# Loads of a selective scan on one Trainium2 core: upper quarters ahead of lower ones, B and C by one transfer each, delta on 72 partitions

## The chip, the cores and the metric

The kernel runs on one core of one Trainium2 chip. The metric is the device time in microseconds (us) from the start to the end of one execution; lower is better. A core has a matrix engine (PE, with PEld for its weight loads), a vector engine (DVE), an activation engine (ACT), GpSimd (POOL) and a sync engine (SP). SP and ACT issue transfers (DMA) on queues of their own, and 16 DMA engines, which all queues share, move the bytes between the device memory (DRAM) and the on-chip memory of 128 partitions. PE writes its results to a second on-chip memory, PSUM[...].

## What is computed

Four layers work on four images of 64x64 positions and 96 channels. The first two layers are a selective scan: each image is projected to E = 192 channels, passed through a depthwise 3x3 convolution, and then read as a sequence of 4096 steps in K = 4 directions (by rows, by columns, and both backwards). For each direction, channel and each of N = 16 states runs a recurrence over the steps:

```
def step(h, inp):
    u, d, b, c = inp
    dA = jnp.exp(d[..., None] * A)
    h = dA * h + d[..., None] * b[:, :, None, :] * u[..., None]
    y = jnp.einsum('bken,bkn->bke', h, c)
    return (h, y)
```

`d` (delta) and `u` depend on the channel and not on the state; `b` and `c` on the state and not on the channel. The four directions' results are summed, normalised, gated and projected back. The last two layers are a linear attention and a quantised feed-forward network on the tokens; the change doesn't touch them.

## The kernel before

**Phases.** The two scan layers, for two pairs of images each, make four phases, which run one after the other. Of each phase there are three parts: a preparation (`prepare`, L148), the scan itself (`scan_phase`, L466) and an end (`finish`, L543). `run` (L696) lets the end of one phase run beside the preparation of the next; a scan phase runs alone. The token layers come last.

**What the preparation leaves in DRAM.** For each chunk of TC = 512 steps (NC = 8 chunks) `steps` (L282) computes delta, delta times u and the rows of B and C, and stores them. An index g of G = 8 stands for direction and image.

- `ph.delta`: delta as the sum of three bf16 parts (NP16 = 3), laid out part, g, channel, step.
- `ph.du`: delta times u in fp32, laid out copy, g, channel, step. There are two copies, stored by ACT's and by SP's queue (L319).
- `ph.bc`: B's and C's 16 rows each, laid out g, row, step; the store is at L301, on ACT's queue, 256 times in all.

**Partitions in the scan.** All 128 partitions hold independent recurrences: partition = 32 a + 4 g + s, where the state is 4 a + s with a and s from 0 to 3. A quarter is the 32 partitions of one a.

**A unit** is 12 channels (EB) of one chunk. A phase has 8 chunks of 16 units, 128 in all, and 12 scans per unit. For each unit:

- SP loads `h` (L381, L391), 128 partitions by 12 channels by 512 steps in fp32, from `ph.du`. Every row of the source goes to four partitions (the four s), by a broadcast in the source. It takes six transfers: for each of three groups of quarters, first channels 0 to 5 and then 6 to 11. The group `(1, 2)` is the two middle quarters, partitions 32 to 95, in one transfer from both copies (768 KB); `(0, 1)` is the lower quarter, partitions 0 to 31, from copy 0 (384 KB), and `(3, 1)` the upper one, partitions 96 to 127, from copy 1 (384 KB). A row is 12 KB.
- SP loads `dlt` (L371), delta's parts for the 12 channels, on 24 partitions (g, part), 12 KB each (288 KB).
- POOL multiplies `h` by B in four slices of three channels (`times_b`, L403), six scans ahead.
- PE spreads one channel of delta over the 128 partitions and adds up its three parts, by a matmul with a matrix of zeros and ones, `rep` (`replicate`, L408), into PSUM; ACT applies exp with A as its scale (`decay`, L414).
- DVE runs the scan in place on `h` (L420), starting from the carry of the chunk before.
- While the next unit is being scanned, PE contracts `h` with C (`contract`, L432; the weights `cw` are made from C by ACT at L354), ACT evicts the result into `d` (L449), and SP stores it (`store`, L457) in four transfers of 48 KB.

**Order.** The scan phase is a hand-written order (`manual_schedule`), so every engine works its queue in the order of the code. On SP this is, at the end of each unit: the four stores of the unit before; then B's load for the next chunk where the unit is the ninth of its chunk, or C's load for the chunk after the next where it is the last; then `load` of the unit three ahead. `h` has four buffers, `dlt` three, B and C two. B and C are four transfers each (`load_states`, L341), one per quarter. At the start of a phase SP issues B, unit 0, C, unit 1, unit 2 and the next C; ACT makes the first 16 pieces of `cw` before its first exp.

**Constants.** `rep` is loaded once as fp32 and cast to bf16 (L94); `constants` (L902) makes it on the host. Only its first 24 rows are used.

Of the kernel before, what the change touches and what calls it, by code (L numbers as in the profile page):

```python
# [9 lines left out]
F32 = mybir.dt.float32  # L10
F16 = mybir.dt.float16
BF16 = mybir.dt.bfloat16
# [12 lines left out]
NS = 16  # L25
R = 6
K = 4
G = 2 * K
PAD = HW + 2
TC = 512  # L30
NC = L // TC
ROWS = TC // HW
EB = 12
NEB = E // EB
ER = EB // 4
PITCH = 2
NP16 = 3
XD = 2 * NS + R + 1
XD2 = 64 + XD
HID = 384  # L40
# [40 lines left out]
class Consts:  # L81
# [9 lines left out]
        self.eps = pool.tile([128, 1], F32, name="eps")  # L91
        self.nc.vector.memset(self.eps, EPS)

    def scans(self, pool):  # L94
        rep = self.load(pool, "rep", [128, 128])
        self.rep = pool.tile([128, 128], BF16, name="rep16")
        self.nc.vector.tensor_copy(self.rep, rep)
        self.perm = self.load(pool, "perm", [128, K, 128])
        self.unit = self.load(pool, "unit", [128, 128])
        self.gmask = self.load(pool, "gmask", [128, G])  # L100
        self.group = self.load(pool, "group", [C, C])
        self.one_row = self.load(pool, "one_row", [XD2, 1])
# [25 lines left out]
class Scans:  # L128
    def __init__(self, tc, ctx, cst, a):
        nc = self.nc = tc.nc  # L130
        self.tc, self.cst, self.a = tc, cst, a

        def pool(name, bufs, **space):
            return ctx.enter_context(tc.tile_pool(name=name, bufs=bufs, **space))

        self.dram = pool("stage", 2, space=DRAM)
        self.keep = pool("keep", 2)
        cst.scans(pool("const_s", 1))

    def bank(self):  # L140
        return self.p_c.tile([128, TC], F32, name="c")
# [6 lines left out]
    def prepare(self, ph):  # L148

        nc, cst, a, pre = self.nc, self.cst, self.a, ph.pre  # L150
        ph.gs = self.keep.tile([C, 2, 2], F32, name="gs", bufs=3)
        ph.delta = [
            self.dram.tile([NP16, G, E, TC], BF16, name="delta", bufs=2 * NC) for _ in range(NC)
        ]


        ph.du = [
            self.dram.tile([2, G, E + PITCH, TC], F32, name="du", bufs=2 * NC) for _ in range(NC)
        ]
        ph.bc = [self.dram.tile([G, 2 * NS, TC], F32, name="bc", bufs=2 * NC) for _ in range(NC)]  # L160
        ph.ud = self.dram.tile([C, 2, HW, 2, 64], F32, name="ud")
        ph.y = self.dram.tile([64, G, 2, 2, NEB, 16 * EB], F32, name="y")
        x = ph.x_in[ph.pair]

        with self.tc.tile_pool(name="prep", bufs=1) as wp, self.tc.tile_pool(
            name="steps", bufs=2
        ) as sp:

            def load(name, shape, at=0):
                t = wp.tile([at + shape[0]] + shape[1:], F32, name=name)  # L170
                nc.sync.dma_start(t[at:], a[pre + name])
                return t

            xp = load("x_proj", [C, 2, 2, XD2])
            dt_w = load("dt_w", [XD2 - 2 * NS, 2, E], at=2 * NS)
            conv_b = load("conv_b", [C, 2])
            ds = load("Ds", [C, 2, K])
            dsum = wp.tile([C, 2], F32, name="dsum")
            nc.vector.tensor_reduce(dsum, ds, mybir.AxisListType.X, ALU.add)
            yield  # L180


            st = wp.tile([C, 2, 8, 6], F32, name="st")
            with self.tc.tile_pool(name="stats", bufs=2) as rp:
                for hl in range(8):
                    raw = rp.tile([C, 8, 2, 64], F32, name="raw")
                    nc.sync.dma_start(raw, x[:, hl * 8 : hl * 8 + 8])
                    for i in range(2):
                        nc.vector.bn_stats(st[:, i, hl], raw[:, :, i])
                    yield  # L190
            for i in range(2):
                mv = wp.tile([C, 2], F32, name="mv")
                nc.vector.bn_aggr(mv, st[:, i].rearrange("p c s -> p (c s)"))
                ps = self.bank()
                nc.tensor.matmul(ps[:C, :1], cst.group, mv[:, 0:1], start=True, stop=True)
                gs = ph.gs[:, i]
                nc.vector.tensor_copy(gs[:, 0:1], ps[:C, :1])
                d = wp.tile([C, 1], F32, name="d")
                nc.vector.tensor_tensor(d, mv[:, 0:1], gs[:, 0:1], ALU.subtract)
                nc.vector.scalar_tensor_tensor(d, d, d, mv[:, 1:2], ALU.mult, ALU.add)  # L200
                ps = self.bank()
                nc.tensor.matmul(ps[:C, :1], cst.group, d, start=True, stop=True)
                ln = wp.tile([C, 2], F32, name="ln")
                neg_rsqrt(nc, cst, ps[:C, :1], ln[:, 0:1], gs[:, 1:2], ln[:, 1:2])
                nc.vector.tensor_scalar_mul(gs[:, 1:2], gs[:, 1:2], -1.0)
                yield
            in_w = wp.tile([C, E], F32, name="in_w")
            nc.sync.dma_start(in_w, a[pre + "in_proj_w"][:, :E])
            taps = wp.tile([C, 9, E], F32, name="taps")
            nc.sync.dma_start(taps, a[pre + "conv_w"].unsqueeze(0).broadcast_to([C, 9, E]))  # L210

            nc.vector.tensor_tensor(
                taps, taps, in_w.unsqueeze(1).broadcast_to([C, 9, E]), ALU.mult
            )

            xc = [wp.tile([C, 2, L], F32, name="xc", bufs=2) for _ in range(2)]
            yield from self.convolve(ph, 0, x, xc[0], taps, conv_b, dsum)
            ph.beside = 0.5
            other = self.convolve(ph, 1, x, xc[1], taps, conv_b, dsum)
            for i in range(2):  # L220
                for c in range(NC):
                    for k in range(2):
                        yield from self.steps(ph, sp, xc[i], xp, dt_w, i, k, c)
                        for _ in range(2):
                            next(other, None)
                            yield
                for _ in other:
                    yield
                ph.beside = 1.7
# [52 lines left out]
    def steps(self, ph, sp, xc, xp, dt_w, i, k, c):  # L282


        nc, cst = self.nc, self.cst
        u = scan_view(xc, k, c)
# [3 lines left out]
        xd = sp.tile([XD2, TC], F32, name="xd")  # L290

        nc.scalar.activation(xd[:XD], ps[:XD], AF.Identity, bias=cst.one_row[:XD])  # L292
        nc.scalar.activation(
# [4 lines left out]
        for back in range(2):  # L298
            at = 64 * back
            g, cc = 2 * (k + 2 * back) + i, NC - 1 - c if back else c  # L300
            nc.scalar.dma_start(ph.bc[cc][g], xd[at : at + 2 * NS])  # L301
            both.append((g, cc, scan_view(xc, k + 2 * back, cc), self.p_d.tile([C, 2, TC], F32, name="d")))
        for m in range(2):
            for back, (_, _, _, ps) in enumerate(both):
# [5 lines left out]
        for g, cc, u, ps in both:  # L310
            delta = sp.tile([C, 2, TC], F32, name="dl")
            parts = sp.tile([C, NP16, 2, TC], BF16, name="parts")
            du = sp.tile([C, 2, TC], F32, name="du_sb")
# [24 lines left out]
        ph.carry = self.keep.tile([128, E], F32, name="carry")  # L338
        ph.b, ph.c, ph.cw = {}, {}, {}

    def load_states(self, t, of):  # L341

        for a in range(4):
            self.nc.sync.dma_start(t[32 * a : 32 * a + 32], of[:, 4 * a : 4 * a + 4])

    def load_b(self, ph, c):
        ph.b[c] = self.units.tile([128, TC], F32, name="b")
        self.load_states(ph.b[c], ph.bc[c][:, :NS])

    def load_c(self, ph, c):  # L350
        ph.c[c] = self.units.tile([128, TC], F32, name="c")
        self.load_states(ph.c[c], ph.bc[c][:, NS:])

    def weights(self, ph, c, op):  # L354

# [15 lines left out]
    def load_delta(self, u):  # L371

        nc, ph = self.nc, u.ph
        u.dl = self.units.tile([NP16 * G, EB, TC], BF16, name="dlt", bufs=3)
        at = u.eb * EB
        nc.sync.dma_start(
            u.dl.rearrange("p e t -> p (e t)"),
            ph.delta[u.c][:, :, at : at + EB].rearrange("n g e t -> g n (e t)"),
        )

    def load(self, u):  # L381

        nc, ph = self.nc, u.ph
        u.h = self.units.tile([128, EB, TC], F32, name="h", bufs=4)
        self.load_delta(u)
        n = EB // 2
        for first, quarters in ((1, 2), (0, 1), (3, 1)):
            for e in range(0, EB, n):
                self.load_quarters(u, e, n, first, quarters)

# [17 lines left out]
    def replicate(self, u, n):  # L408

        u.a[n] = self.p_a.tile([128, TC], F32, name="a")  # L410
        rep = self.cst.rep[: NP16 * G]
        self.nc.tensor.matmul(u.a[n], rep, u.dl[:, n], start=True, stop=True)  # L412

    def decay(self, u, n):  # L414
        at = u.eb * EB + n
# [486 lines left out]
def constants():  # L902

    p = np.arange(128)
    q = np.arange(C)
    rep = (p[:, None] % 32 < NP16 * G) & (p[:, None] % 32 // NP16 == p[None, :] // 4 % G)
    gmask = p[:, None] // 4 % G == np.arange(G)[None, :]


# [74 lines left out]
```

## Time and profile before

Three runs took 12473.74 to 12504.42 us, with a median of 12483.95 us. The profiled execution took 12443.48 us, and its span from the first to the last instruction is 12441.7 us.

| what | value |
|---|---|
| median of three runs | 12483.95 us |
| profiled execution, its span | 12443.48 us, 12441.7 us |
| PE busy | 10107.0 us (81%) |
| DVE busy | 9376.9 us (75%) |
| POOL busy | 7386.0 us (59%) |
| ACT busy | 7185.6 us (58%) |
| the scan on DVE (L423), with and without carry | 6356.7 + 869.6 us |
| B's product on POOL (L406) | 7016.6 us, 3456 ns each |
| the spreading matmul (L412), its weight load | 551 ns, 101 ns each |
| exp on ACT (L416) | 4030.3 us, 662 ns each |
| SP's queue: bytes, packets | 2163.38 MB, 552496 |
| ACT's queue: bytes, packets | 306.26 MB, 328704 |

The shares are means over the whole execution. The four scan phases take up 1909, 1911, 1912 and 1928 us of the span, and the preparations, ends and token layers, in which other engines and other lines set the pace, lie between and after them. The matrix clock is granted at full or at half speed in turn; it averages 0.665 over the span and 0.60 in the scan phases. A busy PE isn't PE at its peak. Idle time of an engine that isn't the bound costs nothing.

### The profile page before, as it was taken

What the parts mean: (1) busy time and instruction counts of PE and PEld (TensorE: products, weight loads), DVE (VectorE), ACT (ScalarE), POOL (GpSimd) and SP (SyncE); (2) the same over time, 40 slices, a digit from 0 to 9 for tenths busy, and PEclk for the clock granted to TensorE, in tenths of its full rate; (3) what the DMA queues carried; (4) which work ended last, traced back from release to release, by engine and by line L of the source; (5) the groups of instructions that cost most, each with busy time, mean ns of one, the idle gap of its engine ahead of it and who ended that gap; (6) DMA issues with size and microseconds to landing.
All of it is one profiled execution on the core that took longest, in us unless ns stands there. A gap on an engine that the chain in (4) does not pass through costs nothing.

```text
span 12441.7 us, 340858 instructions
## 1 busy us (share of the span) xinstructions
PE 10107.0 (81%) x147008; PEld 4972.1 (40%) x147008; DVE 9376.9 (75%) x9235; ACT 7185.6 (58%) x11815; POOL 7386.0 (59%) x2316
## 2 busy tenths in 40 slices
PE   7758888879878888879878888888878888887777
PEld 2224444433334444433334444443334444444333
DVE  2479999963569999982469999992459999993567
ACT  2456666644456666653456666663446666662556
POOL 0159999950149998960139899880129989990000
PEclk8665565669675555659775656558776655557787
DMA  3567676754667676764566777664567666663110
GB/s 92 172 227 247 244 248 247 248 168 140 213 205 246 245 247 244 250 200 128 176 215 244 246 247 249 243 226 125 174 202 249 244 243 245 245 244 122 30 21 11
DMA packets 882704, 2491.45 MB, mean 200 GB/s; under 512 B 279058, under 2 KB 561840, under 8 KB 737456
## 3 DMA queue, kind: packets, MB, share of 16 engines
q1 hardware_dynamic: 552496, 2163.38, 50.6%
q10 hardware_dynamic: 328704, 306.26, 8.5%
q8 instruction: 1158, 18.97, 0.7%
q14 instruction: 346, 2.83, 0.1%
HBM read 1955.42 MB, written 513.80 MB: 198 GB/s over the span
## 4 chain that ended last, share of the span: by engine, by line
DMA 53%; PE 20%; SPq 8%; DVE 7%; ACT 4%; issue 4%; POOL 3%; ACTq 1%; POOLq 0%; DVEq 0%
DMA h<-du 47%; PE c L260 8%; SPq L396 7%; POOL h L406 3%; PE f L591 2%; DVE h L423 2%; PE d L306 2%; DMA yk<-y 1%; PE c L289 1%; PE f L600 1%; POOL parts L320 1%; PE f L682 1%; DMA du<-du_sb 1%; PE y L441 1%; DVE parts L321 1%
## 5 line engine op out<-in xcount | busy, mean ns | idle before, releaser
L406 POOL TENSOR_TENSOR h<-h,b 128x1536 f32<-128x1536 f32 x2048 | 7016.6, 3456 | 780.6 <-DMA h<-du 369.0
L423 DVE TENSOR_TENSOR_SCAN h<-a,carry,h 128x512 f32<-128x512 f32 x5376 | 6356.7, 1259 | 391.8 <-POOL h L406 360.9
L416 ACT ACTIVATE a<-a,a_col 128x512 f32<-128x512 f32 x6144 | 4030.3, 662 | 1966.6 <-PE a L412 1814.4
L441 PEld LDWEIGHTS y<-h,cw 128*32 128x32 f32 x131072 | 2886.3, 145 | 3597.6 <-issue 1606.1
L441 PE MATMUL y<-h,cw 128*32 128x48 f32 x131072 | 3702.1, 269 | 438.0 <-ACT a L416 216.9
L412 PE MATMUL a<-dlt,rep 24*128 24x512 bf16 x6144 | 3319.4, 551 | 884.8 <-DVE h L423 782.1
L320 POOL CAST parts<-dl 96x1024 bf16<-96x1024 f32 x256 | 341.3, 1348 | 3092.1 <-DVE dl L317 2785.6
L316 DVE TENSOR_TENSOR du_sb<-dl,xc 96x1024 f32<-96x1024 f32 x256 | 397.3, 1577 | 1296.2 <-ACT dl L314 1234.8
L453 ACT COPY d<-y 128x384 f32<-128x384 f32 x2048 | 979.6, 478 | 485.7 <-PE y L441 432.7
L260 PE MATMUL c<-xn,taps 96*96 96x512 f32 x2304 | 1034.1, 609 | 73.5 <-DVE xn L245 71.0
L423 DVE TENSOR_TENSOR_SCAN h<-a,h 128x512 f32<-128x512 f32 x768 | 869.6, 1201 | 189.0 <-ACT a L416 110.6
L412 PEld LDWEIGHTS <-rep 24*128 24x128 bf16 x6144 | 471.9, 101 | 903.6 <-issue 451.0
L306 PE MATMUL d<-xd,dt_w 7*96 7x512 f32 x1024 | 520.8, 859 | 254.9 <-ACT xd L292 225.6
L260 PEld LDWEIGHTS c<-xn,taps 96*96 96x96 f32 x2304 | 382.6, 167 | 707.5 <-issue 628.7
L823 POOL MEMSET tn<- 1x4096 f32 x8 | 27.8, 3506 | 865.0 <-PE pa L843 514.7
L267 ACT ACTIVATE xc<-c,conv_b 96x512 f32<-96x512 f32 x128 | 87.3, 682 | 718.1 <-PE c L260 633.2
L591 PE MATMUL f<-yk,perm 128*128 128x384 f32 x1024 | 415.9, 546 | 99.6 <-DMA yk<-y 88.8
L314 ACT ACTIVATE dl<-d 96x1024 f32<-96x1024 f32 x256 | 252.0, 1017 | 400.9 <-DMA delta<-parts 234.5
L321 DVE TENSOR_TENSOR parts<-dl,parts 96x1024 bf16<-96x1024 f32 x256 | 366.9, 1455 | 153.2 <-POOL parts L320 153.1
L289 PE MATMUL c<-xc,x_proj 96*103 96x512 f32 x512 | 420.2, 958 | 4.2 <-ACT xc L267 4.2
L306 PEld LDWEIGHTS d<-xd,dt_w 7*96 7x96 f32 x1024 | 151.7, 212 | 542.4 <-ACT xd L292 295.8
L360 ACT ACTIVATE cw<-c,gmask 128x256 f32<-128x256 f32 x512 | 287.9, 573 | 126.2 <-DMA h<-du 65.9
(114 smaller groups left out, 5650.6 us busy)
## 6 DMA issues: line engine op xcount, KB each, us to landing
h<-du SPq DMA_DIRECT2D x1024, 768.0 KB
h<-du SPq DMA_DIRECT2D x2048, 384.0 KB
delta<-parts ACTq DMA_DIRECT2D x512, 288.0 KB
dlt<-delta SPq DMA_DIRECT2D x512, 288.0 KB
du<-du_sb SPq DMA_DIRECT2D x256, 384.0 KB
du<-du_sb ACTq DMA_DIRECT2D x256, 384.0 KB
y<-d SPq DMA_DIRECT2D x2048, 48.0 KB
yk<-y SPq DMA_DIRECT2D x256, 384.0 KB
```

The costliest lines, as they stand in the source:

```text
L260: nc.tensor.matmul(rows(ps[:C]), taps[:, tap, h * C : (h + 1) * C], xn[:, ROWS * c + dy : ROWS * (c + 1) + dy, dx : dx + HW], start=tap == ...
L289: nc.tensor.matmul(rows(ps[:XD2]), xp[:, k, h], u[:, h], start=h == 0, stop=h == 1)
L306: nc.tensor.matmul(ps[:, m], dt_w[part, k, m * C : (m + 1) * C], xd[part], start=True, stop=True)
L321: nc.vector.tensor_tensor(parts[:, 2], delta, parts[:, 1], ALU.subtract)
L396: self.nc.sync.dma_start(u.h[32 * first : 32 * (first + quarters), e : e + n].rearrange("p e t -> p (e t)"), source.rearrange("a g e t -> ...
L406: self.nc.gpsimd.tensor_tensor(h, h, b, ALU.mult)
L412: self.nc.tensor.matmul(u.a[n], rep, u.dl[:, n], start=True, stop=True)
L416: self.nc.scalar.activation(u.a[n], u.a[n], AF.Exp, scale=u.ph.a_col[:, at : at + 1])
L423: self.nc.vector.tensor_tensor_scan(u.h[:, n], u.a.pop(n), u.h[:, n], 0.0 if u.c == 0 else u.ph.carry[:, at : at + 1], ALU.mult, ALU.add,)
L441: self.nc.tensor.matmul(view(u.y[32 * j : 32 * j + 32], l2 * EB, (8 * EB, 4), (1, EB)), u.ph.cw[u.c][:, l1, 8 * j + l2], view(u.h, 64 * l1 ...
L453: self.nc.scalar.copy(u.d[:, :, :, l1], u.y[:, : 32 * EB].rearrange("p (t h x) -> p t h x", t=4, h=2))
L591: nc.tensor.matmul(ps[:, : 4 * C].rearrange("p (w v e) -> p w v e", w=4, v=nv), cst.perm[:, k], view(t, off, (sw if k < 2 else -sw, 4), (1 ...
```

## The change

It has three parts.

1. `load` takes the upper quarter's two transfers before the lower quarter's.
2. `ph.bc` is laid out as groups of four rows first, then g, then the row in its group (B's four groups, then C's four), so that the 128 rows of B, and those of C, lie one after another in the order of the partitions. B and C are loaded by one transfer each in place of four. The store in the preparation (L301) writes eight pieces of four rows.
3. `dlt` is on 72 partitions: each of the 24 rows is cut in three by channel (channels 0 to 3, 4 to 7, 8 to 11), and a partition holds 4 channels, 4 KB. `rep` has 72 rows and three versions, one for each third; each has ones for that third's rows alone and zeros elsewhere. `replicate` takes the version and the column that belong to its channel. The fp32 copy of `rep` lies in a pool that is given back after the cast.

Nothing else differs: the number of computing instructions and their order are the same, and the bytes loaded into `h`, `dlt`, B and C too.

```diff
+DROWS = 3 * NP16 * G
+DC = EB // 3
...
-    def scans(self, pool):
-        rep = self.load(pool, "rep", [128, 128])
-        self.rep = pool.tile([128, 128], BF16, name="rep16")
-        self.nc.vector.tensor_copy(self.rep, rep)
+    def scans(self, tc, pool):
+        self.rep = pool.tile([DROWS, EB // DC, 128], BF16, name="rep16")
+        with tc.tile_pool(name="rep_f", bufs=1) as once:
+            rep = self.load(once, "rep", [DROWS, EB // DC, 128])
+            self.nc.vector.tensor_copy(self.rep, rep)
...
-        ph.bc = [self.dram.tile([G, 2 * NS, TC], F32, name="bc", bufs=2 * NC) for _ in range(NC)]
+        ph.bc = [self.dram.tile([NS // 2, G, 4, TC], F32, name="bc", bufs=2 * NC) for _ in range(NC)]
...
-            nc.scalar.dma_start(ph.bc[cc][g], xd[at : at + 2 * NS])
+            nc.scalar.dma_start(ph.bc[cc][:, g], xd[at : at + 2 * NS])
...
-    def load_states(self, t, of):
+    def load_states(self, ph, c, first, name):
 
-        for a in range(4):
-            self.nc.sync.dma_start(t[32 * a : 32 * a + 32], of[:, 4 * a : 4 * a + 4])
+        t = self.units.tile([128, TC], F32, name=name)
+        of = ph.bc[c][first : first + NS // 4]
+        self.nc.sync.dma_start(t, of.rearrange("a g s t -> (a g s) t"))
+        return t
 
     def load_b(self, ph, c):
-        ph.b[c] = self.units.tile([128, TC], F32, name="b")
-        self.load_states(ph.b[c], ph.bc[c][:, :NS])
+        ph.b[c] = self.load_states(ph, c, 0, "b")
 
     def load_c(self, ph, c):
-        ph.c[c] = self.units.tile([128, TC], F32, name="c")
-        self.load_states(ph.c[c], ph.bc[c][:, NS:])
+        ph.c[c] = self.load_states(ph, c, NS // 4, "c")
...
-        u.dl = self.units.tile([NP16 * G, EB, TC], BF16, name="dlt", bufs=3)
+        u.dl = self.units.tile([DROWS, DC, TC], BF16, name="dlt", bufs=3)
         at = u.eb * EB
         nc.sync.dma_start(
             u.dl.rearrange("p e t -> p (e t)"),
-            ph.delta[u.c][:, :, at : at + EB].rearrange("n g e t -> g n (e t)"),
+            ph.delta[u.c][:, :, at : at + EB].rearrange(
+                "n g (h e) t -> (n g) h (e t)", h=EB // DC
+            ),
         )
...
-        for first, quarters in ((1, 2), (0, 1), (3, 1)):
+        for first, quarters in ((1, 2), (3, 1), (0, 1)):
...
-        rep = self.cst.rep[: NP16 * G]
-        self.nc.tensor.matmul(u.a[n], rep, u.dl[:, n], start=True, stop=True)
+        h, e = divmod(n, DC)
+        self.nc.tensor.matmul(u.a[n], self.cst.rep[:, h], u.dl[:, e], start=True, stop=True)
...
-    rep = (p[:, None] % 32 < NP16 * G) & (p[:, None] % 32 // NP16 == p[None, :] // 4 % G)
+    r = np.arange(DROWS)[:, None, None]
+    third = np.arange(EB // DC)[None, :, None]
+    rep = (r % 3 == third) & (r // 3 % G == p[None, None, :] // 4 % G)
```

More of the change, by code (lines that the diff above doesn't have):

```diff
@@ L137, in __init__ @@
         self.keep = pool("keep", 2)
-        cst.scans(pool("const_s", 1))
+        cst.scans(tc, pool("const_s", 1))
     def bank(self):
```

## The prediction

> **What bounds the kernel now.** I read the chain of waits first, on the page.
>
> ```profile
> DMA 53%; PE 20%; SPq 8%; DVE 7%; ACT 4%; issue 4%; POOL 3%; ACTq 1%; POOLq 0%; DVEq 0%
> DMA h<-du 47%; PE c L260 8%; SPq L396 7%; POOL h L406 3%; PE f L591 2%; DVE h L423 2%; PE d L306 2%; DMA yk<-y 1%; PE c L289 1%; PE f L600 1%; POOL parts L320 1%; PE f L682 1%; DMA du<-du_sb 1%; PE y L441 1%; DVE parts L321 1%
> ```
>
> Nearly half of the chain is the loading of `h`, although DVE looks full. So, second, busy time in the four scan phases (columns: stretch, length, busy PE, PEld, DVE, ACT, POOL with counts, clock, DMA share, GB/s).
>
> ```profile
> 775.00:2684.00 1909.00, 1621.64 (x34042) 832.57 (x34041) 1805.52 (x1536) 1305.54 (x2268) 1740.52 (x508) 0.60 0.70 245
> 3613.00:5524.00 1911.00, 1624.24 (x34042) 833.32 (x34041) 1806.32 (x1536) 1306.72 (x2269) 1740.56 (x509) 0.60 0.70 244
> 6462.00:8374.00 1912.00, 1625.12 (x34042) 832.86 (x34041) 1806.35 (x1536) 1307.18 (x2268) 1740.75 (x508) 0.60 0.70 244
> 9307.00:11235.00 1928.00, 1626.64 (x34042) 833.21 (x34041) 1806.62 (x1536) 1307.57 (x2267) 1740.52 (x508) 0.60 0.69 242
> ```
>
> A phase has 128 units, so 14.93 us each (1911/128), of which DVE works 14.11. Its idle time over the phases is 7660 − 7225 = 435 us: the most that feeding it better can bring there. Third, where that idle time lies: DVE's timeline, then SP's.
>
> ```profile
> 1018.72 14.21 DVE L423 TENSOR_TENSOR_SCAN h<-a,carry,h 128x512 f32<-128x512 f32 x12 [1.99 <-POOL h L406]
> 1036.00 28.31 DVE L423 TENSOR_TENSOR_SCAN h<-a,carry,h 128x512 f32<-128x512 f32 x24 [3.08 <-ACT d L453]
> ...
> 1170.99 14.21 DVE L423 TENSOR_TENSOR_SCAN h<-a,carry,h 128x512 f32<-128x512 f32 x12 [2.46 <-POOL h L406]
> ```
>
> ```profile
> 1011.32 6.19 SPq L344 DMA_DIRECT2D c<-bc  x4
> ...
> 1146.86 6.19 SPq L344 DMA_DIRECT2D b<-bc  x4
> ...
> 1208.29 0.69 SPq L376 DMA_DIRECT2D dlt<-delta  x1
> 1210.16 6.89 SPq L396 DMA_DIRECT2D h<-du  x6
> ```
>
> The 12 scans of a unit run without a gap; every stop is at a unit's first scan, where POOL's product is late (the ACT named beside 3.08 is only the last semaphore seen), and the long ones (3.08, 2.46) come two units after B's or C's four issues. Fourth, what SP waits for (1000 to 2600 us: sum, times, longest).
>
> ```profile
> SPq L396 <- DMA h<-du: 419.1, 277, 4.0
> SPq L461 <- DMA h<-du: 135.6, 141, 2.8
> SPq L376 <- DMA h<-du: 118.8, 94, 2.8
> ```
>
> SP can't issue before an earlier load lands: a full set is out all the time. Yet the DMA share is 0.70. The last view, narrow windows in one unit (same columns as above), says why.
>
> ```profile
> 1208.00:1211.00 3.00, 2.20 (x55) 1.20 (x55) 3.00 (x3) 1.90 (x4) 3.00 (x1) 1.00 0.55 229
> 1211.00:1213.00 2.00, 2.00 (x62) 1.28 (x53) 2.00 (x3) 1.31 (x3) 0.85 (x2) 1.00 0.92 257
> 1213.00:1214.00 1.00, 0.20 (x2) 0.00 (x0) 1.00 (x2) 0.87 (x2) 1.00 (x1) 1.00 1.00 351
> 1214.00:1216.00 2.00, 1.04 (x33) 0.73 (x32) 1.35 (x2) 1.16 (x2) 2.00 (x2) 0.65 0.91 264
> 1216.00:1218.00 2.00, 2.00 (x42) 0.93 (x35) 2.00 (x2) 1.02 (x2) 2.00 (x1) 0.50 0.80 332
> ```
>
> Before the two-quarter loads go out (1210.16) about half of the engines work, each at 229/(0.55x16) = 26 GB/s. Then all work, but at 257/14.7 = 17.5 and 264/14.6 = 18; from 1216 they are back at 332/12.8 = 26. So many engines at once isn't the trouble; some pair of transfers is.
>
> [...] In SP's order the upper quarter is last and so still draining when the next unit's two-quarter loads start: the 4 us at 18 GB/s fit it. [...]
>
> [...] Collisions: 0.70x16x14.93 = 167 engine-us are busy, 245 GB/s x 14.93 us / 26 = 141 would do[...].
>
> **The change, part by part.**
> - Upper quarters first. Same bytes and issues. [...] Takes up to 1.6 us from a unit; nothing if I have the cause wrong.
> - `dlt`: 24 rows to 72 partitions[...].
> - B and C: four issues become one [...] about 4 us less of SP (6.19 to some 2) where the long stops are. They are a part of the 435.
> - The 72-row replicate (L412, 551 ns) and its weights (101 ns): rows cost nothing by the nearest rows (7x96 weights at L306 212 ns, 96x96 at L260 167). I take 0; the other end is in the rivals. The order of weights within a unit changes nothing; each matmul loads them now.
> - The store of B/C in the preparation (L301): [...] 0 to 40 us. DMA has room there; I take 8.
> - Start of a phase: SP spends 2.92 us on B, 4.72 on C before the second unit's load; C's landing (765.4) holds ACT's weights and the first scan (774.8). About 3 us x 4 = 12 gained, 0 to 20.
> - The constant `rep` grows to 108 KB, once: nothing.
>
> [...] What is late next: DVE itself. POOL has four products, 13.72 us (the timeline's 4 from 1197.36), and in a phase's first chunk DVE needs 13.73, so the two run level. SP's 11 issues are 7.3 us. At half clock PE takes all but 0.2 us of each three scans (3.53), 13.3 us per unit; yet the gapless scans from 1215.70 ran at clock 0.50 for their first 20 us. So DVE's idle time falls from 435 to about 40 (0.08 per unit for jitter and the level first chunk; bounds 0 and 130). Gain 435 − 40 + 12 − 8 = 399: the profiled 12443.5 becomes 12044. The runs' median lies 40 above that profile (12483.95), so 12085.
>
> **Rivals.**
> - A: collisions [...] move to the lower quarter. Then only bytes count: 0.47+0.08 less of 0.85 us idle per unit; 0.3x512 = 154 remain. Gain 435−154+4 = 285: 12200. [...] Against: full speed from 1216 with 13 engines busy.
> - B: it doesn't do what it says: [...] POOL, 0.4 us from the bound, keeps DVE waiting: some 12440-12480, no change.
> - C, slower: the 72-row replicate. If its weight load grows with rows (101 to 303 ns) and isn't hidden, PE has 13.3+12x0.2 = 15.7 us at half clock, 80% of a phase (mean 0.60), so 15.4 on average, +0.45x512 = 230: 12715. It decides from 0.135 us per replicate ((14.93−13.3)/12). Against: 7 rows load no faster than 96.
>
> **Numbers.** Main case 0.66 (12085; its own range 12030 to 12140), A 0.21, B 0.06, C 0.07. Range 12030 to 12220: main and A. A change under 0.3% (37 us) couldn't be told from none. Faster 0.89, same 0.04, slower 0.07.
>
> **What would show it.** DVE idle in a phase down from 104-121 to about 10; DMA share near 0.6 in the phases, windows at full share with 26 GB/s per engine; SP's waits for `h` loads mostly gone; `dlt` matmuls of 72 rows at the old 551 ns; phases of about 1815. Wrong if full-share windows still fall to 18 GB/s per engine, if stops stay at first scans, or if PE's wait for DVE vanishes.

## The result and the profile after

The changed kernel takes 12286.75 us (median of 4 runs, 12247.23 to 12317.0) against 12488.62 for the kernel before in the same session: 0.9836 of its time, 95% interval 0.9806 to 0.9867. It is faster, clear of the noise, but by half of what was forecast (202 us in place of 399), and it lies above the forecast's range. The profiled execution fell from 12443.48 to 12285.39, by 158 us.

The four scan phases, same view and columns as before (stretch, length, busy PE, PEld, DVE, ACT, POOL with counts, clock, DMA share, GB/s):

```profile
775.00:2649.00 1874.00, 1440.33 (x34042) 813.51 (x34040) 1803.58 (x1535) 1276.38 (x2266) 1741.04 (x508) 0.89 0.73 249
3586.00:5456.00 1870.00, 1444.47 (x34042) 813.59 (x34041) 1802.61 (x1536) 1275.89 (x2267) 1742.37 (x509) 0.89 0.73 250
6396.00:8268.00 1872.00, 1442.23 (x34042) 813.05 (x34041) 1802.96 (x1536) 1275.28 (x2265) 1742.00 (x509) 0.90 0.74 249
9205.00:11078.00 1873.00, 1445.31 (x34042) 813.97 (x34041) 1803.81 (x1536) 1276.24 (x2266) 1742.27 (x509) 0.89 0.73 249
```

The phases sum to 7489 us (7660 before), DVE is busy in 7213 of them (7225), so its idle time is 276 us in place of 435. The 159 us of idle time are the whole gain: the other 12 us that the phases lost came back outside them. The share of busy DMA engines went up, from 0.70 to 0.73, where 0.6 was forecast. Per busy engine that is 249/(0.73x16) = 21.3 GB/s, no more than the 245/(0.70x16) = 21.9 before. That is the first sign that the collisions which the prediction meant to remove did not go.

The chain of waits on the page says the same, and its DMA share grew:

```profile
DMA 57%; PE 20%; SPq 9%; DVE 5%; ACT 4%; issue 3%; POOL 1%; ACTq 1%; DVEq 0%; POOLq 0%
DMA h<-du 51%; SPq L401 8%; PE c L263 8%; PE f L596 2%; PE d L309 2%; DMA yk<-y 2%; DMA delta<-parts 1%; PE c L292 1%; PE f L687 1%; PE f L605 1%; DMA du<-du_sb 1%; POOL parts L323 1%; PE f L676 1%; DVE parts L324 1%; PE f L662 1%
```

SP's waits in 1000 to 2600 us (sum, times, longest), which were to be mostly gone:

```profile
SPq L401 <- DMA h<-du: 488.9, 303, 3.6
SPq L379 <- DMA h<-du: 141.2, 109, 3.6
SPq L466 <- DMA h<-du: 77.8, 98, 2.7
```

They sum to 708 us in place of 674. And DVE's timeline (start, length, what, count, idle time before it) still has its stops where POOL's product is late, only smaller: in 1000 to 2640 us there were 13 of 2.5 us or more (up to 4.03) and there is one now (2.53), and the pattern two units after B's and C's issues no longer stands out. Two of the stops that stayed:

```profile
1046.39 28.53 DVE L428 TENSOR_TENSOR_SCAN h<-a,carry,h 128x512 f32<-128x512 f32 x24 [1.62 <-POOL h L411]
1075.38 28.31 DVE L428 TENSOR_TENSOR_SCAN h<-a,carry,h 128x512 f32<-128x512 f32 x24 [0.47 <-POOL h L411]
```

The narrow windows of one unit show where the speed is lost now. First SP's timeline, then the windows with the columns of the phases:

```profile
1196.33 0.81 SPq L379 DMA_DIRECT2D dlt<-delta  x1
1198.20 8.74 SPq L401 DMA_DIRECT2D h<-du  x6
```

```profile
1196.00:1198.00 2.00, 1.20 (x34) 0.67 (x32) 2.00 (x2) 1.54 (x3) 2.00 (x2) 1.00 0.53 217
1198.00:1200.00 2.00, 1.70 (x42) 0.91 (x35) 2.00 (x3) 1.31 (x4) 2.00 (x1) 1.00 0.94 245
1200.00:1202.00 2.00, 1.51 (x38) 0.79 (x37) 2.00 (x3) 1.11 (x2) 0.54 (x2) 1.00 0.83 319
1202.00:1204.00 2.00, 1.22 (x34) 0.79 (x34) 2.00 (x3) 1.71 (x3) 2.00 (x1) 1.00 0.81 236
```

With about half of the engines busy: 217/(0.53x16) = 25.6 GB/s each, as before. With `dlt` and the two-quarter loads under way: 245/(0.94x16) = 16.3. Later in the same unit 236/(0.81x16) = 18.2 once more. A full share at 16 to 18 GB/s per engine was named beforehand as what would show the forecast wrong.

### The profile page after: what moved, and what is told of

Its sections match the earlier page's. It is cut to its first block, busy times and chain, and to the rows that moved or that the text cites. A ratio compares the mean times of both kernels' runs of the same rounds, so it can differ in the third digit from the quotient of the medians.

```text
span 12283.6 us, 340681 instructions
## 1 busy us (share of the span) xinstructions
PE 9393.5 (76%) x147008; PEld 4897.8 (40%) x147008; DVE 9369.7 (76%) x9235; ACT 7066.9 (58%) x11815; POOL 7389.7 (60%) x2316
## 4 chain that ended last, share of the span: by engine, by line
DMA 57%; PE 20%; SPq 9%; DVE 5%; ACT 4%; issue 3%; POOL 1%; ACTq 1%; DVEq 0%; POOLq 0%
DMA h<-du 51%; SPq L401 8%; PE c L263 8%; PE f L596 2%; PE d L309 2%; DMA yk<-y 2%; DMA delta<-parts 1%; PE c L292 1%; PE f L687 1%; PE f L605 1%; DMA du<-du_sb 1%; POOL parts L323 1%; PE f L676 1%; DVE parts L324 1%; PE f L662 1%
## 5 line engine op out<-in xcount | busy, mean ns | idle before, releaser
L446 PEld LDWEIGHTS y<-h,cw 128*32 128x32 f32 x131072 | 2789.8, 129 | 3520.4 <-issue 1302.1
L446 PE MATMUL y<-h,cw 128*32 128x48 f32 x131072 | 3663.3, 266 | 537.8 <-DVE h L428 210.6
L417 PE MATMUL a<-dlt,rep 72*128 72x512 bf16 x6144 | 2562.4, 428 | 1339.9 <-DVE h L428 1242.8
L417 PEld LDWEIGHTS <-rep 72*128 72x128 bf16 x6144 | 490.8, 99 | 888.7 <-issue 646.5
```

The costliest lines, as they stand in the source:

```text
L417: self.nc.tensor.matmul(u.a[n], self.cst.rep[:, h], u.dl[:, e], start=True, stop=True)
L446: self.nc.tensor.matmul(view(u.y[32 * j : 32 * j + 32], l2 * EB, (8 * EB, 4), (1, EB)), u.ph.cw[u.c][:, l1, 8 * j + l2], view(u.h, 64 * l1 ...
```

## Experiments

Each ratio is to the kernel before in the same session, with its 95% interval. The sessions (the changed kernel; e1 to e4; e5 to e8; e9 to e12; e13 and e14; e15 and e16) ran on several chips, and the kernel before took 12445 to 12489 us in them, so a difference in us across sessions can be off by some tens of us. A point below is a hundredth of the time of the kernel before. "Last quarter" is the one that SP loads last in each unit, and "B, C" the number of issues for each load of B or C. "Half" means partitions 0 to 63 or 64 to 127. The last two columns are read in one and the same window of the first scan phase, 1100 to 2500 us: DVE's idle time in it, and GB/s per busy DMA engine, worked out as GB/s over (share x 16).

| kernel | last quarter | delta: rows, piece, first partition | B, C | median us | ratio (interval) | DVE idle | GB/s per engine |
|---|---|---|---|---|---|---|---|
| before | upper | 24, 12 KB, 0 | 4 issues | 12488.62 | 1 | 80 | 22.1 |
| changed | lower | 72, 4 KB, 0 | 1 | 12286.75 | 0.9836 (0.9806-0.9867) | 52 | 21.3 |
| e12, changed again | lower | 72, 4 KB, 0 | 1 | 12278.99 | 0.9846 (0.9829-0.9862) | 56 | 21.2 |
| e1 | lower | 24, 12 KB, 0 | 4 | 12695.47 | 1.0199 (1.018-1.0218) | 114 | 21.7 |
| e2 | lower | 24, 12 KB, 0 | 1 | 12797.52 | 1.027 (1.0254-1.0285) | 137 | 21.0 |
| e3 | upper | 72, 4 KB, 0 | 1 | 12188.73 | 0.9781 (0.9767-0.9796) | 44 | 21.7 |
| e4 | lower | 48, 6 KB, 64 | 1 | 11997.56 | 0.9627 (0.9613-0.9642) | 0 | 21.7 |
| e5 | lower | 24, 12 KB, 64 | 4 | 12757.57 | 1.0253 (1.0238-1.0268) | 134 | 20.5 |
| e6 | upper | 24, 12 KB, 64 | 4 | 13250.9 | 1.0649 (1.0633-1.0665) | 200 | 19.4 |
| e7 | lower | 48, 6 KB, 0 | 1 | 11975.61 | 0.9624 (0.9608-0.964) | 0 | 22.8 |
| e8 | upper | 48, 6 KB, 64 | 1 | 12608.53 | 1.0131 (1.0114-1.0148) | 107 | 20.6 |
| e9 | upper | 24, 12 KB, 0 | 1 | 12413.52 | 0.9954 (0.9939-0.9968) | 76 | 21.7 |
| e10 | upper | 48, 6 KB, 0 | 1 | 11956.6 | 0.9586 (0.9572-0.96) | 0 | 22.8 |
| e11 | lower | 48, 6 KB, 2 | 1 | 12066.3 | 0.9674 (0.966-0.9689) | 11 | 21.7 |
| e13 | upper | none | 4 | 12099.84 | 0.9735 (0.9697-0.9772) | 0 | 23.3 |
| e14 | lower | none | 4 | 11965.05 | 0.9601 (0.9586-0.9615) | 0 | 22.6 |
| e15 | upper | 32, 12 KB, 0 | 4 | 12366.13 | 0.9933 (0.9918-0.9948) | 51 | 23.5 |
| e16 | lower | 96, 3 KB, 0 | 1 | 12107.3 | 0.9719 (0.9698-0.9739) | 24 | 21.8 |

### The parts one by one: e1, e2, e9, e3

e1 is the kernel before with the order alone:

```diff
-        for first, quarters in ((1, 2), (0, 1), (3, 1)):
+        for first, quarters in ((1, 2), (3, 1), (0, 1)):
```

> The kernel before, with the order of the quarters changed and nothing else. Two theories. [...] in the changed kernel the slow stretches only moved to delta's pieces[...]. Then the order alone takes the slow stretches away: [...] only the stops behind B's and C's four issues stay: about 12210 us, windows of full share at 25 GB/s per engine or more. Load: [...]. Then the order does nothing: within 0.3% of before, 12450 to 12520.

e2 is the changed kernel with delta back on 24 partitions:

```diff
-DROWS = 3 * NP16 * G
-DC = EB // 3
+DROWS = NP16 * G
+DC = EB
...
-                "n g (h e) t -> (n g) h (e t)", h=EB // DC
+                "n g e t -> g n (e t)"
...
-    rep = (r % 3 == third) & (r // 3 % G == p[None, None, :] // 4 % G)
+    rep = (r // NP16 == p[None, None, :] // 4 % G) & (third == 0)
```

> The changed kernel with delta back on 24 partitions in rows of 12 KB; order and single B and C transfers stay. [...] DVE idle about 10 us a phase: 12095 us, clearly faster than the changed kernel. Load: [...] the same slow stretches: slower than the changed kernel, 12350 or more.

e9 is the kernel before with B's and C's single transfers and their layout in DRAM alone (the lines of the change to `ph.bc`, its store, and `load_states`).

> The kernel before with B and C by one transfer each (layout, store and load) and nothing else. If the stops behind B's and C's issues go as the prediction says, some 100 us faster than before: 12320 to 12400. [...] the stops only spread over the other units: 12420 to 12470.

e3 is the changed kernel with e1's line turned round: lower quarter first again.

> The changed kernel with the lower quarter loaded ahead of the upper one again; delta on 72 partitions and single B and C transfers stay. [...] the two-quarter loads collide with the upper quarter again (1.6 us), [...]: about the changed kernel's time, 12240 to 12340. Load: the order is without effect: the changed kernel's time, 12250 to 12320. This run tells the two apart less by its time than by its windows[...].

The order alone costs 2.0%, 238 us: the step on which most of the forecast rested has the wrong sign here, and neither theory of e1's forecast had a slower kernel in it. (Both were suppositions of mine, and no view shows either: in the first, two transfers into the same half slow each other; in the second, "load", more transfers at once are slower, whatever they write.) In the changed kernel too it costs: 0.9781 without it (e3, faster than both of its forecasts), 0.9846 with it (e12). B and C alone bring 0.46%, 59 us, between the two ranges of e9's forecast. With the order already changed they brought nothing; e2 is even 102 us slower than e1, which these runs leave unexplained. Nearly all that pays is delta's layout: from e2 to the changed kernel 1.027 falls to 0.984.

In e1 the slow stretch comes with the two-quarter loads, issued at 1203.10 after `dlt` at 1201.24:

```profile
1200.00:1203.00 3.00, 2.80 (x65) 1.34 (x55) 3.00 (x4) 2.06 (x4) 3.00 (x1) 0.50 0.54 220
1203.00:1205.00 2.00, 2.00 (x54) 1.21 (x57) 2.00 (x3) 1.17 (x3) 0.36 (x1) 0.50 0.79 220
1205.00:1207.00 2.00, 1.63 (x26) 0.43 (x18) 2.00 (x3) 1.65 (x4) 0.85 (x1) 0.50 0.90 233
```

220/(0.54x16) = 25.5 GB/s per engine, then 220/(0.79x16) = 17.4 and 233/(0.90x16) = 16.2. With the upper quarter no longer at the end, the dip is there all the same. So the pair of transfers that I had named is not the only one that collides, if it does at all.

### Which half delta is in: e5, e6

If the quarter that still drains when delta arrives matters, moving delta to the other half must turn the order's effect round. e5 is e1, e6 the kernel before, both with delta's 24 rows on partitions 64 to 87:

```diff
-        u.dl = self.units.tile([NP16 * G, EB, TC], BF16, name="dlt", bufs=3)
+        u.dl = self.units.tile([64 + NP16 * G, EB, TC], BF16, name="dlt", bufs=3)
...
-            u.dl.rearrange("p e t -> p (e t)"),
+            u.dl[64:].rearrange("p e t -> p (e t)"),
...
-        rep = self.cst.rep[: NP16 * G]
-        self.nc.tensor.matmul(u.a[n], rep, u.dl[:, n], start=True, stop=True)
+        rep = self.cst.rep[64 : 64 + NP16 * G]
+        self.nc.tensor.matmul(u.a[n], rep, u.dl[64:, n], start=True, stop=True)
```

> The kernel before (delta on 24 partitions, rows of 12 KB, B and C by four transfers) with the upper quarter first and delta's 24 rows on partitions 64-87 in place of 0-23. Neighbours theory: [...] the cost comes where delta and the quarter just ahead of it are in the same half. The order alone (12695) put the lower quarter beside delta on 0-23. With delta on 64-87 the two are in different halves: clearly faster than 12695, about 12250 to 12460. Order theory: the upper quarter first is bad by itself, or delta's place is of no account: 12650 to 12740.

> The kernel before with delta's 24 rows on partitions 64-87 and the old order (upper quarter last). Neighbours theory: now the upper quarter, 96-127, stands just ahead of delta in the same half: slower than before by 100 us or more, 12560 to 12800. Order theory: the order is that of before, so is the time: 12440 to 12480.

```profile
1100.00:2500.00 1400.00, 1128.18 (x22646) 563.35 (x22646) 1200.19 (x1014) 882.89 (x1520) 1153.61 (x338) 0.51 0.72 224
```

That is e6: more engines busy than before (0.72), fewer bytes (224 GB/s), DVE idle for 200 of 1400 us. The four kernels make a two-by-two table:

| | upper quarter last | lower quarter last |
|---|---|---|
| delta on 0-23 | 1 | 1.0199 |
| delta on 64-87 | 1.0649 | 1.0253 |

With delta below, the new order costs 2.0 points; with delta above, the same line brings 4.0. The reads from DRAM are the same in both rows of the table, so the reversal comes from the partitions that delta is written to. (The matmul reads delta there too, but DVE's stops in e6 are put down to POOL's product, 1065 of 1094 us, as in the kernel before.) Half the difference of the two, 3.0 points or some 370 us, is what it costs, in an additive reading, when delta follows a quarter of its own half. That reading is a fit to four numbers, and where the two transfers meet isn't shown. What is left is a gain of 1.0 point for the new order itself, which would fit the pair that the forecast named, and a cost of 3.5 points for delta in the upper half. For that one there is a candidate: delta in 64 to 87 stands directly ahead of the two-quarter loads, which write 64 to 95 too. No run tests it. So e5's direction against e6 came as expected and the levels didn't: e5 was to fall below the kernel before or to about it and is 2.5% above it, and e6 is 450 us above the end of its range.

### No delta at all: e13, e14

The kernel before and e1, with delta's loads left out after the first three units of a phase (later units compute with old decays):

```diff
+        n = u.c * NEB + u.eb
+        if n == 0:
+            self.dlts = [
+                self.units.tile([NP16 * G, EB, TC], BF16, name="dlt", bufs=3) for _ in range(3)
+            ]
+        u.dl = self.dlts[n % 3]
+        if n >= 3:
+            return
```

> The kernel before with delta's loads left out after the first three units of a phase: all later units use those three units' delta, so the scan's numbers are others[...]. [...] (the slow stretches are the upper quarter against the middle quarters' upper half): they stay, 18 GB/s per busy engine when the two-quarter loads start, 22 over a phase. Delta theory (delta's rows[...] make most of them): they are mostly gone, 24 GB/s per busy engine or more over a phase. Both: DVE is the bound or nearly, 11950 to 12100.

> The same with the upper quarter first. [...] no slow stretches now, 25 GB/s per busy engine over a phase, against 22 with the old order. Delta theory: as with the old order, within 1 GB/s. An own cost of the new order, without delta: slower than the run with the old order by 50 us or more.

Without delta the new order is faster, 0.9601 against 0.9735. The phases of e13:

```profile
772.00:2566.00 1794.00, 1519.04 (x34043) 819.79 (x34042) 1793.48 (x1537) 1279.27 (x2269) 1739.68 (x508) 0.73 0.65 240
3498.00:5345.00 1847.00, 1573.32 (x34051) 829.10 (x34054) 1803.25 (x1537) 1290.10 (x2268) 1741.13 (x508) 0.67 0.70 233
```

The third and fourth phase repeat the pair (1793 and 1848 us). In e14 all four take 1793 to 1795; its first two:

```profile
774.00:2567.00 1793.00, 1518.30 (x34042) 820.27 (x34041) 1793.00 (x1537) 1279.06 (x2268) 1740.05 (x508) 0.74 0.66 240
3506.00:5299.00 1793.00, 1522.65 (x34042) 821.53 (x34041) 1793.00 (x1536) 1279.23 (x2268) 1740.06 (x509) 0.73 0.66 240
```

So without delta the old order loses some 54 us in every other phase, at a share of 0.70 for 233 GB/s (20.8 per engine), and the new order doesn't. That is a loss of the kind that the prediction named; but in the first and third phase the same old order loses nothing, and why the phases differ isn't known, so the pair that the prediction blamed isn't shown as the cause. What is shown is that the sign of the order depends on whether delta is loaded (leaving it out also takes away one issue of SP per unit). The rates decide nothing: for e13 the theories had 22 GB/s per engine (the prediction's pair) and 24 or more (delta), and its phases have 23.1 and 20.8; for e14 the first of them had 25, and it has 22.7. The 26 that the forecast took for all loads belongs to stretches in which about half of the engines work.

### The number of rows and where they begin: e4, e7, e8, e10, e11

e4 is the changed kernel with delta split in two (48 rows of 6 KB) and put on partitions 64 to 111; in e7 the same rows lie on 0 to 47:

```diff
-DROWS = 3 * NP16 * G
-DC = EB // 3
+DROWS = 2 * NP16 * G
+DC = EB // 2
+DAT = 64
...
-        u.dl = self.units.tile([DROWS, DC, TC], BF16, name="dlt", bufs=3)
+        u.dl = self.units.tile([DAT + DROWS, DC, TC], BF16, name="dlt", bufs=3)
...
-            u.dl.rearrange("p e t -> p (e t)"),
+            u.dl[DAT:].rearrange("p e t -> p (e t)"),
...
-        self.nc.tensor.matmul(u.a[n], self.cst.rep[:, h], u.dl[:, e], start=True, stop=True)
+        self.nc.tensor.matmul(u.a[n], self.cst.rep[DAT:, h], u.dl[DAT:, e], start=True, stop=True)
```

e7 has `DAT = 0`; e8 is e4 and e10 is e7 with the lower quarter first again.

> The changed kernel with delta's rows split in two, not three, on 48 partitions from 64 to 111 (pieces of 6 KB[...]). [...] 12095 us. Load: [...]: 12250 to 12320.

> The kernel of 11998 us (upper quarter first, delta in 48 rows of 6 KB on partitions 64-111, single B and C) with the 48 rows on partitions 0-47, nothing else changed[...]. Neighbours theory: [...]: slower than 11998, 12080 to 12290. Pieces theory (6 KB in place of 4 KB is what made that kernel fast): unchanged, 11980 to 12020.

> The kernel of 11998 us with the lower quarter first again, delta's 48 rows staying on partitions 64-111. Neighbours theory: the upper quarter is now ahead of delta's rows and of the middle quarters' upper half, all three in partitions 64-127: slower, 12080 to 12300. Order theory: upper first is what cost 2% alone and 0.5% in the changed kernel, so taking it back gains or, where DVE is the bound already, changes nothing: 11950 to 12020.

> The kernel of 11976 us with the lower quarter first again. It asks whether the order brings what the prediction said, now that delta doesn't disturb: if the upper quarter as the last one collides with the middle quarters' upper half, it is slower, 12050 to 12250; if the order is without worth, or bad by itself, 11950 to 12000.

e4, e7 and e10 take nearly all of DVE's idle time away, e4 and e7 whatever the half. e8, where delta follows a quarter of its own half, the upper one, is 611 us slower than e4, more than its forecast had, so the two-by-two pattern is there with 48 rows too, on one side. On the other side it isn't seen: e7, whose delta follows the lower quarter in the lower half, was to be slower than e4 by the neighbours theory and isn't. e7 and e10 both stand at DVE's floor, which can hide a cost, but they also move the same 263 GB/s at the same share of 0.72. e10 came in the range for an order without worth. So the cost of a neighbour in the same half isn't a general rule. e10 is the fastest of all. Two of its phases:

```profile
774.00:2568.00 1794.00, 1420.08 (x34046) 806.30 (x34046) 1793.46 (x1537) 1266.13 (x2269) 1743.40 (x509) 0.91 0.71 260
3507.00:5301.00 1794.00, 1425.73 (x34055) 807.66 (x34058) 1793.48 (x1537) 1265.01 (x2269) 1742.98 (x509) 0.90 0.71 260
```

DVE is busy in 3586.94 of 3588 us; its own work is the bound. SP's waits (1000 to 2500 us) turned round:

```profile
SPq L468 <- ACT a L423: 550.4, 104, 6.8
SPq L403 <- DMA h<-du: 113.3, 99, 3.1
```

SP now waits mostly to store results, for work of the engines, and for landed loads of `h` only some 118 us in all.

What do 48 rows have that 24 and 72 lack? Two theories were put to e11. By that of the pieces, 6 KB are better than 4 or 12 KB wherever the rows lie. By that of the alignment, it counts how many rows there are and on which partition they begin; that was a supposition of mine. The trace names no row and no engine of a transfer, so only speeds can tell. e11 moves e7's rows by two partitions, to 2 to 49, and keeps pieces, bytes and order (its matmul has two more rows, of zeros, and the three buffers are set up once a phase):

```diff
-DAT = 0
+DAT = 2
...
-        u.dl = self.units.tile([DAT + DROWS, DC, TC], BF16, name="dlt", bufs=3)
+        u.dl = self.dlts[(u.c * NEB + u.eb) % 3]
...
+                for t in self.dlts:
+                    nc.vector.memset(t[: max(DAT, 1)], 0.0)
```

> The kernel of 11976 us (upper quarter first, delta in 48 rows of 6 KB on partitions 0-47) with the 48 rows two partitions further on, 2 to 49, in buffers whose first two partitions are set to zero once a phase[...]. Alignment theory: [...] Then it is slower by 100 us or more, 12080 to 12400. Pieces theory (48 pieces of 6 KB are better than 72 of 4 KB or 24 of 12 KB wherever they lie): 11970 to 12000.

e7, then e11, in the window of the table:

```profile
1100.00:2500.00 1400.00, 1112.51 (x26600) 631.23 (x26599) 1400.00 (x1193) 985.72 (x1768) 1366.87 (x399) 0.91 0.72 263
1100.00:2500.00 1400.00, 1103.83 (x26355) 625.63 (x26359) 1388.72 (x1180) 978.26 (x1754) 1348.50 (x395) 0.91 0.75 260
```

Two partitions cost 91 us by the medians of two sessions (0.9624 to 0.9674, or 62 us by the ratios): the engines are busy for 0.75 with 260 GB/s, against 0.72 with 263 in e7, and DVE waits again. The spans of the two profiles are 11970.1 and 12067.7 us. That is the direction of the alignment theory, a little short of the 100 us that it asked for, and against the pieces theory; since e7 stands at DVE's floor, the cost may be larger than what shows.

### The number of rows, or the size of the pieces: e15, e16

e16 is the changed kernel with delta split in four: the bytes of the 72 rows on 96, in pieces smaller still. e15 is the kernel before with a zero plane stored beside delta's three, so that the pieces of 12 KB stay and there are 32 rows in place of 24, a third more bytes.

```diff
-DROWS = 3 * NP16 * G
-DC = EB // 3
+DROWS = 4 * NP16 * G
+DC = EB // 4
...
-    rep = (r % 3 == third) & (r // 3 % G == p[None, None, :] // 4 % G)
+    rep = (r % 4 == third) & (r // 4 % G == p[None, None, :] // 4 % G)
```

```diff
-            self.dram.tile([NP16, G, E, TC], BF16, name="delta", bufs=2 * NC) for _ in range(NC)
+            self.dram.tile([NP16 + 1, G, E, TC], BF16, name="delta", bufs=2 * NC) for _ in range(NC)
...
+                nc.scalar.dma_start(ph.delta[cc][NP16, g, h * C : (h + 1) * C], self.cst.zero)
...
-        u.dl = self.units.tile([NP16 * G, EB, TC], BF16, name="dlt", bufs=3)
+        u.dl = self.units.tile([4 * G, EB, TC], BF16, name="dlt", bufs=3)
```

> The changed kernel with delta's rows split in four instead of three: 96 rows in pieces of 3 KB; [...] same order and B/C. [...] Alignment theory: near the 48 rows, 11950 to 12050, DMA share about 0.72 and DVE at its floor of some 1794 us per phase. Piece theory (what separates 72 from 48 rows is 4 KB against 6 KB pieces): no better than the changed kernel, 12280 to 12400.

> The kernel before with a fourth, zero plane beside the three of delta, so that 32 rows in place of 24 are loaded in the same pieces of 12 KB[...]. The preparation also stores the zero plane. Bytes theory: [...] 12650 to 12750. Alignment theory: [...] in spite of the bytes: under 12400.

The kernel before, then e15, then e16, in the window of the table:

```profile
1100.00:2500.00 1400.00, 1190.18 (x24953) 610.25 (x24946) 1320.21 (x1118) 958.29 (x1671) 1275.37 (x373) 0.60 0.70 247
1100.00:2500.00 1400.00, 1116.74 (x25574) 612.41 (x25566) 1348.71 (x1146) 960.86 (x1711) 1307.48 (x382) 0.80 0.69 259
```

```profile
1100.00:2500.00 1400.00, 1085.12 (x26072) 619.57 (x26075) 1375.55 (x1169) 970.50 (x1740) 1332.46 (x389) 0.93 0.74 258
```

e15 moves 96 KB more per unit, stores more in the preparation, and is still 0.67% faster than the kernel before: 259 GB/s at a share of 0.69, where 247 took 0.70. Its first scan starts at 799.90 us in place of 774.79, so the longer preparation takes a part of the gain back. By its bytes alone it was to take 12650 to 12750 us. But 32 rows also lie on more partitions than 24, and that wider spread may have a part in it. e16 is 172 us faster than the changed kernel with pieces of 3 KB, where the theory of the pieces had it no faster; it doesn't reach the 11950 to 12050 that alignment alone called for. So 96 rows in place of 72, in smaller pieces, bring 172 of the 303 us between 72 rows (e12, 12279) and 48 rows (e7, 11976), all across sessions; by what, these runs don't show. The other 131 are open: the pieces are half as large as those of e7, and the rows from 64 up lie in the other half. No run separates these. The matrix clock moved with the rows too, 0.60 to 0.80 in e15 and 0.89 to 0.93 in e16, and no run keeps it still there; in e11 and e7 it is the same, 0.91, and e8, at 0.84, has more idle time of DVE than the kernel before at 0.60.

e12 is the changed kernel once more, beside e9 to e11, and repeats its result:

> The changed kernel itself once more, beside the others on one chip: 12250 to 12300, so that the lower quarter first (12189) is really the faster order with delta on 72 partitions.

## Why the prediction was wrong, by its own steps

- **The bound: right, its limit a little low.** What feeding DVE better could bring was 435 us of idle time, and the changed kernel gained just the 159 us by which it fell. e10 takes 430 of them: its phases sum to 7180 us with DVE busy in 7175. DVE's busy time fell by 50 us as well, which the 435 left out.
- **Upper quarters first, "takes up to 1.6 us from a unit": the step that failed.** It comes to the 26 engine-us of the collisions (167 less 141) over 16 engines, put down to the one pair that I looked for, the upper quarter's tail against the next unit's two-quarter loads. Alone the new order costs 238 us (e1), where up to 1.6x512 us would have been a gain; inside the changed kernel it costs 0.65 points, some 80 us (e3 against e12). The speed per busy engine didn't rise (21.9 to 21.3 GB/s). The new order puts the lower quarter directly ahead of delta, whose rows lie in the same half; that this neighbour is what costs fits the reversal in e5 and e6 and the gain in e14, and is not shown beyond that. The trace of before could have raised the doubt: the dip at 1211 came when `dlt`, issued at 1208.29, was under way as well, and I gave all of it to the other pair. "Nothing if I have the cause wrong" was too narrow a lower end: a reordering that makes one pair of transfers strangers makes another pair neighbours.
- **26 GB/s for all bytes.** Even without delta the engines go at 21 to 23 over a phase (e13, e14); 26 was seen with about half of them busy, and in one short stretch with 13. The forecast's times per transfer, 0.47 us for `dlt` and 0.08 us for B and C among them, were my estimates from this rate and from a share of the bytes for each engine, which no view shows; so was the step to DVE as what is late next.
- **dlt, 0.47 us: right in sign, mis-sized.** From e2 to the changed kernel it is (12797.52 - 12286.75)/512 = 1.0 us per unit, across two sessions. Its bytes alone don't explain it: e15 with more of them is faster than the kernel before. The 72 rows were also a poor number: 48 give 303 us more (e7 against e12), and 96, with the bytes of the 72, give 172 (e16).
- **B and C:** 0.08 us per unit and the long stops were more than measured: 59 us alone (e9). There stops of up to 3.0 us stayed, four of 2.5 us or more; in the changed kernel one of 2.5 did.
- **The 72-row replicate:** right that its rows cost nothing on the path, wrong in its time. It was to stay at 551 ns, and took 428, while the granted clock in the phases rose from 0.60 to 0.89:

```profile
L417 PE MATMUL a<-dlt,rep 72*128 72x512 bf16 x6144 | 2562.4, 428 | 1339.9 <-DVE h L428 1242.8
```

- **Start of a phase and the B/C store:** the first scan of the program came 1.4 us earlier (774.79 to 773.38), not 3, and the stretches outside the phases grew by 13 us where the two terms together gave -4. The room that the forecast saw for the store was there: between the first two phases the share of busy DMA engines is 0.54, before and after. DVE's busy time in the phases fell by 12, which cancels it.
- **The rivals:** A came nearest ("move to the lower quarter"), but kept 154 us of idle time where 276 stayed, since it had nothing for a cost of the new order. C fell: weight loads of 72 rows take 99 ns. No rival had a slower order: that part alone ends on the other side.

## What to carry to other kernels

When transfers compete, a new order has to be judged by every pair that it brings together, not by the pair that it parts (here the order alone cost 238 us, e1); runs with the suspect transfer left out, in both orders, tell cheaply whether it turns the sign. Try other numbers of rows and other first partitions for a load, by splitting rows or even by loading a few useless ones: here 48 rows took nearly all idle time away (e7, e10), a shift by two partitions gave some of it back (62 to 91 us, e11), and 32 rows in place of 24 brought 0.67% (e15). A rate seen while half of the engines work is not a rate for all of them: here 26 GB/s per engine became 21 to 23.

## What was not expected of the hardware

- The number of delta's rows and the partition on which they begin: 33% more bytes of delta in 0.67% less time (e15), and 62 to 91 us for a shift by two partitions (e11).
- Delta's half and the quarter ahead of it: 4.0 points of time from one reordered line with delta above (e6 to e5), with the opposite sign below.
- PE's granted clock in the window was higher with more rows in the replicate, 0.60 (24), 0.80 (32), 0.91 (48), 0.89 (72), 0.93 (96), and its matmul was shorter though it has more rows: 551 ns with 24 rows, 457 with 32, 425 with 48 (e7), 428 with 72. Other kernels with 24 rows have 0.51 to 0.58, without delta's loads 0.72, and e8 with 48 has 0.84, so rows are not all of it. DVE's stops are put down to POOL's product and not to PE, and the cause of the clock was not looked for.
